# Layer 0 of a two-layer image network: how the last 42 channels are laid over the partitions

## The chip, the cores and the metric

The kernel runs on one core of a Trainium2 chip, in single precision. The metric is the time of one execution on the device, in microseconds (us), and the median of several executions. A core has five engines that run side by side, each through its own list of instructions in order: TensorE (PE in the profile; its weight loads are PEld) multiplies matrices, VectorE (DVE) and ScalarE (ACT) work on elements, GpSimd (POOL) does a little of the same, and SyncE (SP) issues the DMA transfers. Engines wait for each other by semaphores. TensorE writes to PSUM, a memory of 128 partitions and eight banks; everything else lies in SBUF, with 128 partitions too. A matmul takes a weight block (contracted rows on the partitions, by output columns) and a moving block, and writes its output columns to PSUM partitions.

## The reference, cut to what matters

The input x has shape (4, 64, 256, 256): four images of 64 channels. The change lies in layer 0 alone:

```
x = x + L0(gn(x))                     # gn: normalise by groups of 2 channels

h = einsum('oi,bihw->bohw', w_in, x)  # 64 -> 3 * 170 channels
gate, x_sp, x_fr = split(h, 3, axis=1)
sp = depthwise conv 3x3 of x_sp with w_dw, padding SAME
f  = rfft2 of x_fr in 8x8 patches, times fft_weight
fr = irfft2(f)
fused = gelu(gate) * (sp + fr)
L0 = einsum('oi,bihw->bohw', w_out, fused)   # 170 -> 64 channels
```

Layer 1, which follows, normalises again and runs two bidirectional state-space scans, along rows and along columns, with a feed-forward part. Nothing of it is touched.

## The kernel before

Layer 0 goes through each image in 32 strips of eight rows, 128 strips in all. The 170 hidden channels fall into groups of 64, 64 and 42. The first two groups ("a") share the partitions, and their convolution is done as products on TensorE (products). The group of 42 ("b") is laid out so that both halves of the partitions hold the same 42 channels (padded to 64) for different rows of the strip, and its 3x3 convolution is nine multiply-and-add instructions ("taps") over 128 partitions: the first by ScalarE, the other eight by VectorE (tap_b, L858).

The rows of x come in by parity. load_rows (L653) loads into at[0:64] every second row from one above the strip, and into at[64:128] the rows between; er holds the same kind of rows without the shift, and en is er normalised. Group b keeps this order before the change: one partition half has the strip's even rows, the other its odd ones.

The steps of group b are these. inputs_b (L751) multiplies at by xb, which holds the weights of the filter input on a block diagonal, in four matmuls over all 128 rows to 64 columns, 512 wide; half of each weight block is zero. ScalarE copies the result to rows 1 to 4 of xat, and two DMAs copy shifted rows of each half to the other half of a second tile, xen, from which taps 3, 4 and 5 (the middle row of the filter) read. Row 0 of xat is the last row of the strip before, copied by ScalarE in normal_rows (L681). gate_b (L847) does the same for the gate with gw, from en, and ScalarE puts its Gelu into geb. inverse_b (L831) turns the spectrum back with the table qi2, and add_b (L843) adds it to the taps' sum, acc. fuse_b (L869) multiplies with geb, and project (L875) multiplies acc by w_out and adds the part of the other groups in the same PSUM tile, from which residual (L888) adds er.

The strips overlap. The loop at L944 writes out one order of work by hand for the strip at hand (cur), the next (ahead) and the one before (behind); the instructions of TensorE, VectorE and ScalarE keep that order on their queues (mm at L203, vec and act at L161). The order of the DMAs on SyncE's queue is left to the framework's scheduler. Within an iteration it begins with tap 0, and the parts that matter here stand in this order: products of the first half with spec1 of the next strip, gate_a, inverse_b, project of the strip before, inverse_a, spec2 of the next strip (parts 0 and 1), products of the second half, inverse_a, gate_b, inputs_b of the next strip, tap 5, spec2 of the next strip (part 2).

PSUM is full: two tiles of two banks each for the products (m14, m23), and two rotating buffers of two banks under the name "two", which every other matmul of the loop uses in turn. A step that takes a "two" waits until the step two before it has been read out by ScalarE or VectorE.

Of the kernel before, what the change touches and what calls it, by code (L numbers as in the profile page):

```python
# [11 lines left out]
AF = mybir.ActivationFunctionType  # L12
ALU = mybir.AluOpType
# [3 lines left out]
C = 64  # L17
HID = 170
S = 256
P = 128  # L20
# [38 lines left out]
def _constants():  # L59

    out = np.zeros((P, CONST_N), np.float64)

    def put(name, a):
        o, w = CONST_AT[name]
        out[: a.shape[0], o : o + w] = a

    eye = np.eye(P)
    swap = np.roll(eye, C, axis=0)
    put("ident", eye)
    put("swap", swap)  # L70
    put("nswap", -swap)
    put("cen", eye - np.kron(np.eye(2), np.full((C, C), 1.0 / C)))
    pair = np.kron(np.eye(C // 2), np.ones((2, 2)))
    put("gm", np.kron(np.ones((2, 2)), pair) / 4.0)
    put("on2", np.kron(np.eye(2, 34, 2), np.full((C, 1), 1.0 / C)))
    put("sgn", np.concatenate([-np.ones((C, 1)), np.ones((C, 1))]))

    r, c = np.meshgrid(np.arange(8), np.arange(8), indexing="ij")  # L80
    q, sel = [], []
    for k1 in range(8):
        for k2 in range(5):
            own = k1 in (0, 4) and k2 in (0, 4)
            if k2 in (0, 4) and k1 > 4:
                continue
            w = np.zeros(40)
            w[k1 * 5 + k2] += 0.5
            w[((8 - k1) % 8 if k2 in (0, 4) else k1) * 5 + k2] += 0.5
            ang = 2 * np.pi * (k1 * r + k2 * c) / 8  # L90
            q.append(np.cos(ang).ravel() / 8 * (1 if own else math.sqrt(2)))
            sel.append(w)
            if not own:
                q.append(np.sin(ang).ravel() / 8 * math.sqrt(2))
                sel.append(w)
    q, sel = np.array(q), np.array(sel)
    assert q.shape == (64, 64) and np.allclose(q @ q.T, np.eye(64))
    put("qf", np.concatenate([q.T, q.T]))
    qi2 = np.zeros((2, 64, 2, 4, 2, 8))
    for pc in range(2):  # L100
        qi2[pc, :, :, :, pc] = q.reshape(64, 4, 2, 8).transpose(0, 2, 1, 3)
    put("qi2", qi2.reshape(128, 128))
    put("qj", qi2.reshape(128, 2, 4, 8, 2).transpose(0, 1, 4, 2, 3).reshape(128, 128))
    put("selt", np.concatenate([sel, sel]).T)
    return out.astype(np.float32)

# [2 lines left out]
def tile_kernel(ctx: ExitStack, tc: tile.TileContext, x, cst, w0, winp, wdwp, w1, out):  # L109
    nc = tc.nc  # L110
    nb = x.shape[0]

    def new(pool, shape, tag, bufs=None, dt=F32):
        return pool.tile(shape, dt, tag=tag, name=tag, **({} if bufs is None else {"bufs": bufs}))
# [49 lines left out]
    vec, act, gps = InOrder(nc.vector), InOrder(nc.scalar), InOrder(nc.gpsimd)  # L164
# [27 lines left out]
    with ExitStack() as l0:  # L192
# [10 lines left out]
        def mm(*args, **kw):  # L203

            tc.keep_in_program_order(nc.tensor.matmul(*args, **kw))  # L205

        gw = wt0("gw").rearrange("p (g m) -> p g m", g=3)
        ow = wt0("ow").rearrange("p (g m) -> p g m", g=3)
        ga, oa = new(wp, [P, P], "ga"), new(wp, [P, C], "oa")
        for h in range(2):  # L210
            p = slice(h * C, (h + 1) * C)
# [5 lines left out]
        xb = new(wp, [P, P], "xb")  # L217
        taps = new(wp, [P, 9], "taps")
        with tc.tile_pool(name="prep0", bufs=1) as prep:
# [4 lines left out]
            lo, hi, every = slice(0, C), slice(C, P), slice(0, P)  # L224
# [26 lines left out]
        with tc.tile_pool(name="pssp", bufs=1, space=PSUM) as pp:  # L251
            ps = new(pp, [P, 512], "sp")
# [380 lines left out]


        ats = [new(ld, [P, 5, S + 2], f"at{k}", 1) for k in range(3)]
        xats = [new(wk, [P, 5, S + 2], f"xat{k}", 1) for k in range(2)]
        for t in ats + xats:
            nc.gpsimd.memset(t[:, :, 0 : S + 2 : S + 1], 0.0)

# [41 lines left out]
        def normal_rows(n):  # L681
            t = strips[n]
            b, s, at = t["b"], t["s"], t["at"]
            if s == 0:
                out_stats[b] = new(wk, [P, 2 * NS0, 6], "stats2")
            lo, hi = (1 if s == 0 else 0), (4 if s == NS0 - 1 else 5)
            normalise(at[:, lo:hi, 1 : S + 1], at[:, lo:hi, 1 : S + 1], b)
            if s == 0:
                nc.gpsimd.memset(at[0:C, 0, 1 : S + 1], 0.0)
                normalise(at[C:P, 0, 1 : S + 1], at[C:P, 0, 1 : S + 1], b, slice(C, P))  # L690
            if s == NS0 - 1:
                nc.gpsimd.memset(at[C:P, 4, 1 : S + 1], 0.0)  # L692
                normalise(at[0:C, 4, 1 : S + 1], at[0:C, 4, 1 : S + 1], b, slice(0, C))
            en = t["en"] = new(wk, [P, 4, S], "en")
            normalise(en, t["er"], b)

            v14 = t["v"] = new(wk, [P, 5, S], "v14")
            t["v14"], t["v23"] = v14.rearrange("p r (c k) -> p r k c", k=2), new(wk, [P, 5, 2, 128], "v23")
            t["xat"], t["xen"] = xats[n % 2], new(wk, [P, 4, S + 2], "xen")
            t["hw"], t["stats2"] = hws[n % 2], out_stats[b]  # L700
            if s > 0:
                act.copy(t["xat"][:, 0], strips[n - 1]["xat"][:, 4])

        def outer_in(t):

# [44 lines left out]

        def inputs_b(t):  # L751

            if t["s"] == 0:
                ps = new(pp, [P, 2, 512], "two").rearrange("p q (r c) -> p (q r) c", c=S)
                mm(ps[:, 0], lhsT=xb, rhs=t["at"][:, 0, 1 : S + 1], start=True, stop=True)
                act.copy(t["xat"][:, 0, 1 : S + 1], ps[:, 0])
            ps = new(pp, [P, 2, 512], "two").rearrange("p q (r c) -> p (q r) c", c=S)
            for i in range(2):
                for h in range(2):
                    p = slice(h * C, (h + 1) * C)  # L760
                    mm(
                        ps[p, 2 * i : 2 * i + 2], lhsT=xb[:, p], rhs=t["at"][:, 1 + 2 * i : 3 + 2 * i, 1 : S + 1],
                        start=True, stop=True,
                    )
            act.copy(t["xat"][:, 1:5, 1 : S + 1], ps)
            for k in range(2):
                nc.sync.dma_start(out=t["xen"][k * C : (k + 1) * C], in_=t["xat"][(1 - k) * C : (2 - k) * C, k : k + 4])

        def products(t, half, name, third):

# [43 lines left out]
        def outer(t, half):  # L814
            y = t["y", half] = t.pop("y").rearrange("p e k x -> p (e k x)")
            vec.tensor_tensor(y, t.pop("m14").rearrange("p e k m c -> p (e k m c)"), y, ALU.add)
# [28 lines left out]
            vec.tensor_tensor(o, t.pop("fr").rearrange("p f (m c) -> p f m c", m=4), o, ALU.add)  # L845

        def gate_b(t):  # L847
            ps = new(pp, [P, 2, 512], "two").rearrange("p q (r c) -> p (q r) c", c=S)
            for i in range(2):
                for h in range(2):  # L850
                    p = slice(h * C, (h + 1) * C)
                    mm(
                        ps[p, 2 * i : 2 * i + 2], lhsT=gw[:, 2, p], rhs=t["en"][:, 2 * i : 2 * i + 2, :], start=True, stop=True
                    )
            t["geb"] = new(wk, [P, 4, S], "geb", 1)
            act.activation(t["geb"], ps, AF.Gelu)

        def tap_b(t, k):  # L858
            dy, dx = k // 3, k % 3
            src = (t["xat"][:, 0:4], t["xen"], t["xat"][:, 1:5])[dy]  # L860
            if k == 0:
                t["acc"] = new(wk, [P, 4, S], "acc")
                act.activation(t["acc"], src[:, :, dx : dx + S], AF.Copy, scale=taps[:, 0:1])
                return
            vec.scalar_tensor_tensor(
                t["acc"], src[:, :, dx : dx + S], taps[:, k : k + 1], t["acc"], ALU.mult, ALU.add
            )

        def fuse_b(t):  # L869
            vec.tensor_tensor(t["acc"], t["acc"], t["geb"], ALU.mult)  # L870
# [1 line left out]
        def split(v, half):  # L872
            return v.rearrange("p m (c k) -> p k m c", k=2)[:, :, :, half * 64 : (half + 1) * 64]

        def project(t):  # L875
            po = t["po"] = new(pp, [P, 2, 512], "two")
            for half in range(2):
                fu = t.pop(("fu", half))
                for e in range(2):
                    p = slice(e * C, (e + 1) * C)  # L880
                    mm(
                        po[p, half].rearrange("p (k m c) -> p k m c", k=2, m=4), lhsT=ow[:, 2, p], rhs=split(t["acc"], half),
                        start=True, stop=False,
                    )
                for e in range(2):
                    mm(po[e * C : (e + 1) * C, half], lhsT=oa, rhs=fu[:, e], start=False, stop=True)

# [56 lines left out]
        for b in range(nb):  # L944
            if b + 1 < nb:
                nxt_stats = new(wk, [P, 2 * NS0, 6], "stats1")
            for s in range(NS0):
# [11 lines left out]
                def ahead(step, *args):  # L959
                    if nxt is not None:  # L960
                        step(nxt, *args)
# [37 lines left out]
                behind(finish, 0)  # L999
                inverse_a(cur, 0)  # L1000
                outer(cur, 0)
                ahead(spec2, 0)
                ahead(spec2, 1)
                behind(finish, 1)
# [12 lines left out]
                inverse_a(cur, 1)  # L1017
                outer(cur, 1)
                gate_b(cur)
                ahead(inputs_b)  # L1020
                tap_b(cur, 5)
                ahead(spec2, 2)
                if s == NS0 - 3 and b + 1 < nb:
# [600 lines left out]
```

## Time and profile before

| | us |
|---|---|
| median of 3 runs | 9118.38 |
| lowest and highest run | 9117.01, 9126.76 |
| the profiled execution's own time | 9128.26 |
| its span | 9126.5 |
| first and last tap 0 of layer 0 in it, from the span's start | 182.1, 4146.2 |
| VectorE, one tap (128 partitions, 1024 elements) | 1.28 |
| ScalarE, copy of the filter input to xat | 1.02 |
| DMA of xen, two per strip, 258 KB each, from issue to landing | 4.8 |

The profile lists one execution, instruction by instruction. A row of the view in order of time gives the start from the span's start, the length, the engine, the source line, the operation, what is written and read (by the names of the tiles), the shapes, and how many instructions were merged. Matmuls overlap, so the length of a merged run of matmuls is longer than what it adds; from the start of one run to the start of the next is what it takes. L205 and L301 are the lines of the helpers that record matmuls and VectorE's operations, so rows are told apart by their tiles. One row covers instructions of the same kind that follow without a pause.

### The profile page before, as it was taken

Reading aid. Unit: us, or ns where it says so; the run is one execution under the profiler, and the core shown is the slowest. Engines: PE = TensorE matmul, PEld = TensorE weight load, DVE = VectorE, ACT = ScalarE, POOL = GpSimd, SP = SyncE. Lnnn points to the kernel's source line nnn. Section 1 sums busy time; section 2 is a strip of 40 time slices with the busy share of each in tenths; the row PEclk is TensorE's granted clock in tenths of the full one; section 3 lists DMA queues with packets and bytes.
Section 4 is the critical chain, followed back from the end, with each engine's and each line's share of the span. In section 5 each row is a group of like instructions: output and inputs, shape, how many; then the busy total and the mean of one; then the engine's idle time right before and its main releaser. Section 6 shows DMA issues by size and latency. Waiting matters only on the chain. (4 is left out here: it accounts for less than half of the span.)

```text
span 9126.5 us, 182410 instructions
## 1 busy us (share of the span) xinstructions
PE 8613.1 (94%) x78454; PEld 5705.4 (63%) x78454; DVE 7105.8 (78%) x8837; ACT 3460.7 (38%) x5218; POOL 2406.8 (26%) x1278
## 2 busy tenths in 40 slices
PE   3999999999999999998899988999978999889999
PEld 2666666666666666665566656566655666555666
DVE  7999999999999998896766756677756677567676
ACT  3444444444444444445422236222254222352222
POOL 3000000000000000003734435544446444455443
PEclk9999999999999999999999999999999999999999
DMA  7444444444444333334423335233253233451332
GB/s 175 107 107 107 104 105 110 109 103 105 108 107 107 92 93 87 91 85 134 147 57 88 85 103 177 73 80 88 70 170 113 70 89 80 117 187 40 88 84 70
DMA packets 655573, 938.37 MB, mean 103 GB/s; under 512 B 43184, under 2 KB 584880, under 8 KB 619184
## 3 DMA queue, kind: packets, MB, share of 16 engines
q1 hardware_dynamic: 654768, 926.71, 38.3%
q8 instruction: 618, 10.13, 0.5%
q14 instruction: 187, 1.53, 0.1%
HBM read 583.86 MB, written 275.05 MB: 94 GB/s over the span
## 5 line engine op out<-in xcount | busy, mean ns | idle before, releaser
L205 PE MATMUL m<-v,sw 64*128 64x256 f32 (+1 forms) x8192 | 1538.6, 392 | 0.1
L205 PEld LDWEIGHTS m<-v,sw 64*128 64x128 f32 (+1 forms) x8192 | 1120.0, 187 | 503.2 <-issue 360.0
L1439 POOL TENSOR_TENSOR xr<-xr,fx 128x512 f32<-128x512 f32 x512 | 651.5, 1272 | 1864.4 <-ACT xr L1438 1375.5
L1344 PE MATMUL pst<-fx,wb 64*128 64x256 f32 (+1 forms) x4992 | 1019.8, 438 | 37.8 <-DVE stm L301 18.3
L692 POOL MEMSET at<- 64x256 f32 x4 | 1.2, 308 | 3685.1 <-PE two L205 3685.1
L301 DVE SCALAR_TENSOR_TENSOR acc<-xat,taps,acc 128x1024 f32<-128x1024 f32 x640 | 820.6, 1282 | 15.3 <-ACT acc L162 1.6
L1344 PEld LDWEIGHTS pst<-fx,wb 64*128 64x128 f32 (+1 forms) x4992 | 508.9, 187 | 374.6 <-issue 245.3
L1469 POOL TENSOR_TENSOR rs<-ve,mhalf 128x32 f32<-128x32 f32 x128 | 695.5, 5434 | 100.5 <-DVE ve L301 100.5
L162 ACT ACTIVATE ge<-two 128x1024 f32<-128x1024 f32 x256 | 262.7, 1026 | 1080.1 <-PE two L205 1080.0
L301 DVE SCALAR_TENSOR_TENSOR stm<-stm,step,pst 128x512 f32<-128x512 f32 x640 | 478.6, 748 | 232.5 <-PE pst L1344 219.0
L1440 ACT ACTIVATE sq<-xr 128x512 f32<-128x512 f32 x512 | 323.4, 632 | 876.4 <-POOL xr L1439 876.4
L205 PEld LDWEIGHTS m<-ct,hw 128*64 128x64 f32 x16384 | 509.3, 138 | 118.1 <-issue 118.1
L301 DVE SCALAR_TENSOR_TENSOR sto<-sto,step,pst 128x512 f32<-128x512 f32 x512 | 382.9, 748 | 242.5 <-PE pst L1344 231.2
L1344 PE MATMUL px<-wb,xr 128*128 128x128 f32 x4096 | 567.8, 282 | 0.0
L301 DVE TENSOR_TENSOR z<-xc,pr 128x512 f32<-128x512 f32 x256 | 265.1, 1037 | 386.2 <-PE pr L1100 378.8
L301 DVE TENSOR_TENSOR hw<-two,wsp 128x1020 f32<-128x1020 f32 (+1 forms) x384 | 422.7, 1101 | 176.0 <-PE two L205 162.7
L1344 PEld LDWEIGHTS px<-wb,xr 128*128 128x128 f32 x4096 | 518.0, 192 | 54.2 <-issue 41.8
L301 DVE TENSOR_TENSOR y<-px,rs 128x512 f32<-128x512 f32 x512 | 354.2, 692 | 226.5 <-PE px L1344 217.2
L1344 PE MATMUL ph<-sto,wb 128*64 128x128 f32 (+1 forms) x5120 | 528.0, 299 | 0.0
L205 PE MATMUL m<-ct,hw 128*64 128x64 f32 x16384 | 527.1, 223 | 0.0
L1344 PE MATMUL ph<-stm,wb 128*64 128x128 f32 (+1 forms) x5120 | 525.0, 299 | 0.0
L1344 PEld LDWEIGHTS ph<-stm,wb 128*64 128x64 f32 (+1 forms) x5120 | 408.9, 147 | 144.6 <-issue 128.0
(317 smaller groups left out, 16420.7 us busy)
## 6 DMA issues: line engine op xcount, KB each, us to landing
strip<-x1d SPq DMA_DIRECT2D x512, 256.0 KB, 7.5
fx<-fxd SPq DMA_DIRECT2D x128, 1024.0 KB, 7.0
at<-in_x_dram SPq DMA_DIRECT2D x248, 320.0 KB, 5.4
xen<-xat SPq DMA_DIRECT2D x256, 258.0 KB, 4.8
sx<-in_x_dram SPq DMA_DIRECT2D x256, 256.0 KB, 4.0
pr<-in_x_dram SPq DMA_DIRECT2D x256, 256.0 KB, 4.1
er<-in_x_dram SPq DMA_DIRECT2D x256, 256.0 KB, 4.1
x1d<-x SPq DMA_DIRECT2D x256, 256.0 KB, 4.0
```

Source lines behind the costliest of these rows:

```text
L162: return lambda *args, **kw: tc.keep_in_program_order(getattr(self.engine, name)(*args, **kw))
L205: tc.keep_in_program_order(nc.tensor.matmul(*args, **kw))
L301: tc.keep_in_program_order(getattr(nc.vector, name)(*args, **kw))
L692: nc.gpsimd.memset(at[C:P, 4, 1 : S + 1], 0.0)
L1344: tc.keep_in_program_order(nc.tensor.matmul(*args, **kw))
L1439: nc.gpsimd.tensor_tensor(xr, xr, fx, ALU.add)
L1440: nc.scalar.activation(sq, xr, AF.Square)
L1469: nc.gpsimd.tensor_tensor(r, ve.rearrange("p n c -> p (n c)"), mhalf, ALU.pow)
```

## The change

Group b now lies by half of the strip: the lower partition half holds the first four of eight consecutive rows, the upper half the last four. Since at and en hold rows by parity, each matmul of inputs_b and gate_b now takes one parity's half of the partitions (64 rows) and writes to one half of the output partitions (64 columns), two rows at a time: four 64x64 tiles, each with its own quarter of the array, the two parities in two banks. ScalarE's copy and Gelu interleave the two parities as they write. xat grows from five rows to six, with two rows of overlap at its top: the upper half gets them from the lower half's last rows, the lower half from the upper half of the strip before, each by a DMA. All nine taps now read xat at a row offset, so xen and its two DMAs go, and so does ScalarE's copy of one row. In project, acc is no longer in er's order, so each matmul with the b weights splits in two of half the width, by the partition half that holds the rows. The table qi2 is reordered to match. In the loop, inputs_b of the next strip moves up, from after gate_b to ahead of spec2 (part 0).

```
-        xats = [new(wk, [P, 5, S + 2], f"xat{k}", 1) for k in range(2)]
+        xats = [new(wk, [P, 6, S + 2], f"xat{k}", 1) for k in range(2)]
...
-            t["xat"], t["xen"] = xats[n % 2], new(wk, [P, 4, S + 2], "xen")
+            t["xat"], t["last"] = xats[n % 2], xats[1 - n % 2]
...
-            if s > 0:
-                act.copy(t["xat"][:, 0], strips[n - 1]["xat"][:, 4])
...
         def inputs_b(t):
+            xat = t["xat"]
+            lo, hi = slice(0, C), slice(C, P)
...
+                nc.sync.dma_start(out=xat[lo, 0:2], in_=t["last"][hi, 4:6])
...
-            for i in range(2):
-                for h in range(2):
-                    p = slice(h * C, (h + 1) * C)
+            for e in range(2):
+                for o in range(2):
+                    p = slice(e * C, (e + 1) * C)
                     mm(
-                        ps[p, 2 * i : 2 * i + 2], lhsT=xb[:, p], rhs=t["at"][:, 1 + 2 * i : 3 + 2 * i, 1 : S + 1],
+                        ps[o * C : (o + 1) * C, e], lhsT=xb[p, p], rhs=t["at"][p, 1 + 2 * o : 3 + 2 * o, 1 : S + 1],
                         start=True, stop=True,
                     )
-            act.copy(t["xat"][:, 1:5, 1 : S + 1], ps)
-            for k in range(2):
-                nc.sync.dma_start(out=t["xen"][k * C : (k + 1) * C], in_=t["xat"][(1 - k) * C : (2 - k) * C, k : k + 4])
+            act.copy(
+                xat[:, 2:6, 1 : S + 1].rearrange("p (j e) c -> p e j c", e=2), ps.rearrange("p e (j c) -> p e j c", j=2)
+            )
+            nc.sync.dma_start(out=xat[hi, 0:2], in_=xat[lo, 4:6])
...
         def gate_b(t):
...
-                        ps[p, 2 * i : 2 * i + 2], lhsT=gw[:, 2, p], rhs=t["en"][:, 2 * i : 2 * i + 2, :], start=True, stop=True
+                        ps[o * C : (o + 1) * C, e], lhsT=gw[p, 2, p], rhs=t["en"][p, 2 * o : 2 * o + 2, :], start=True, stop=True
...
         def tap_b(t, k):
-            src = (t["xat"][:, 0:4], t["xen"], t["xat"][:, 1:5])[dy]
+            src = t["xat"][:, dy : dy + 4, dx : dx + S]
...
         def project(t):
...
-                for e in range(2):
-                    p = slice(e * C, (e + 1) * C)
-                    mm(
-                        po[p, half].rearrange("p (k m c) -> p k m c", k=2, m=4), lhsT=ow[:, 2, p], rhs=split(t["acc"], half),
-                        start=True, stop=False,
-                    )
+                for h in range(2):
+                    for e in range(2):
+                        mm(
+                            po[e * C : (e + 1) * C, half].rearrange("p (k m c) -> p k m c", k=2, m=4)[:, :, 2 * h : 2 * h + 2],
+                            lhsT=ow[:, 2, h * C : (h + 1) * C], rhs=split(t["acc"][:, e::2], half), start=(h == 0), stop=False,
+                        )
...
                 outer(cur, 0)
+                ahead(inputs_b)
                 ahead(spec2, 0)
                 ahead(spec2, 1)
...
                 gate_b(cur)
-                ahead(inputs_b)
                 tap_b(cur, 5)
                 ahead(spec2, 2)
```

More of the change, by code (lines that the diff above doesn't have):

```diff
@@ L101, in _constants @@
         qi2[pc, :, :, :, pc] = q.reshape(64, 4, 2, 8).transpose(0, 2, 1, 3)
+    put("qj", qi2.reshape(128, 2, 4, 8, 2).transpose(0, 1, 4, 2, 3).reshape(128, 128))
+    for pc in range(2):
+        qi2[pc, :, :, :, pc] = q.reshape(64, 2, 4, 8)
     put("qi2", qi2.reshape(128, 128))
-    put("qj", qi2.reshape(128, 2, 4, 8, 2).transpose(0, 1, 4, 2, 3).reshape(128, 128))
     put("selt", np.concatenate([sel, sel]).T)
@@ L751, in inputs_b @@
         def inputs_b(t):
+            xat = t["xat"]
+            lo, hi = slice(0, C), slice(C, P)
             if t["s"] == 0:
[L754 to L757, printed above, removed]
-            for i in range(2):
-                for h in range(2):
-                    p = slice(h * C, (h + 1) * C)
+                ps = new(pp, [P, 2, 512], "two")
+                mm(ps[lo, 0, :S], lhsT=xb[hi, hi], rhs=t["at"][hi, 0, 1 : S + 1], start=True, stop=True)
+                act.copy(xat[lo, 1, 1 : S + 1], ps[lo, 0, :S])
+                nc.gpsimd.memset(xat[lo, 0, 1 : S + 1], 0.0)
+            else:
+                nc.sync.dma_start(out=xat[lo, 0:2], in_=t["last"][hi, 4:6])
+            ps = new(pp, [P, 2, 512], "two")
+            for e in range(2):
+                for o in range(2):
+                    p = slice(e * C, (e + 1) * C)
                     mm(
-                        ps[p, 2 * i : 2 * i + 2], lhsT=xb[:, p], rhs=t["at"][:, 1 + 2 * i : 3 + 2 * i, 1 : S + 1],
+                        ps[o * C : (o + 1) * C, e], lhsT=xb[p, p], rhs=t["at"][p, 1 + 2 * o : 3 + 2 * o, 1 : S + 1],
                         start=True, stop=True,
                     )
-            act.copy(t["xat"][:, 1:5, 1 : S + 1], ps)
-            for k in range(2):
-                nc.sync.dma_start(out=t["xen"][k * C : (k + 1) * C], in_=t["xat"][(1 - k) * C : (2 - k) * C, k : k + 4])
+            act.copy(
+                xat[:, 2:6, 1 : S + 1].rearrange("p (j e) c -> p e j c", e=2), ps.rearrange("p e (j c) -> p e j c", j=2)
+            )
+            nc.sync.dma_start(out=xat[hi, 0:2], in_=xat[lo, 4:6])
         def products(t, half, name, third):
@@ L847, in gate_b @@
         def gate_b(t):
[L848 to L851, printed above, removed]
+            ps = new(pp, [P, 2, 512], "two")
+            for e in range(2):
+                for o in range(2):
+                    p = slice(e * C, (e + 1) * C)
                     mm(
-                        ps[p, 2 * i : 2 * i + 2], lhsT=gw[:, 2, p], rhs=t["en"][:, 2 * i : 2 * i + 2, :], start=True, stop=True
+                        ps[o * C : (o + 1) * C, e], lhsT=gw[p, 2, p], rhs=t["en"][p, 2 * o : 2 * o + 2, :], start=True, stop=True
                     )
             t["geb"] = new(wk, [P, 4, S], "geb", 1)
-            act.activation(t["geb"], ps, AF.Gelu)
+            act.activation(
+                t["geb"].rearrange("p (j e) c -> p e j c", e=2), ps.rearrange("p e (j c) -> p e j c", j=2), AF.Gelu
+            )
         def tap_b(t, k):
             dy, dx = k // 3, k % 3
-            src = (t["xat"][:, 0:4], t["xen"], t["xat"][:, 1:5])[dy]
+            src = t["xat"][:, dy : dy + 4, dx : dx + S]
             if k == 0:
                 t["acc"] = new(wk, [P, 4, S], "acc")
-                act.activation(t["acc"], src[:, :, dx : dx + S], AF.Copy, scale=taps[:, 0:1])
+                act.activation(t["acc"], src, AF.Copy, scale=taps[:, 0:1])
                 return
-            vec.scalar_tensor_tensor(
-                t["acc"], src[:, :, dx : dx + S], taps[:, k : k + 1], t["acc"], ALU.mult, ALU.add
-            )
+            vec.scalar_tensor_tensor(t["acc"], src, taps[:, k : k + 1], t["acc"], ALU.mult, ALU.add)
         def fuse_b(t):
@@ L878, in project @@
                 fu = t.pop(("fu", half))
-                for e in range(2):
-                    p = slice(e * C, (e + 1) * C)
-                    mm(
-                        po[p, half].rearrange("p (k m c) -> p k m c", k=2, m=4), lhsT=ow[:, 2, p], rhs=split(t["acc"], half),
-                        start=True, stop=False,
-                    )
+                for h in range(2):
+                    for e in range(2):
+                        mm(
+                            po[e * C : (e + 1) * C, half].rearrange("p (k m c) -> p k m c", k=2, m=4)[:, :, 2 * h : 2 * h + 2],
+                            lhsT=ow[:, 2, h * C : (h + 1) * C], rhs=split(t["acc"][:, e::2], half), start=(h == 0), stop=False,
+                        )
                 for e in range(2):
```

## The prediction, made before the changed kernel was run

> **What bounds it now.** I read the page first, then busy time by stretch, then one strip in order of time on each engine, then the waits. The page (busy time, share of the span, instructions) says TensorE, with VectorE second:
>
> ```profile
> span 9126.5 us, 182410 instructions
> PE 8613.1 (94%) x78454; PEld 5705.4 (63%) x78454; DVE 7105.8 (78%) x8837; ACT 3460.7 (38%) x5218; POOL 2406.8 (26%) x1278
> ```
>
> The busy times by stretch (length, then PE, PEld, DVE, ACT, POOL, granted clock, DMA share, GB/s), one row per image of layer 0; images one, three and four:
>
> ```profile
> 182.00:1176.00 994.00, 988.51 (x11226) 652.89 (x11226) 923.10 (x958) 423.52 (x480) 1.19 (x3) 1.00 0.45 108
> ...
> 2173.00:3170.00 997.00, 992.41 (x11240) 652.64 (x11240) 927.24 (x963) 423.05 (x479) 1.17 (x3) 1.00 0.43 105
> 3170.00:4180.00 1010.00, 1004.84 (x11348) 660.43 (x11345) 904.78 (x911) 421.33 (x477) 0.31 (x1) 1.00 0.35 85
> ```
>
> TensorE is busy 99.5% at full clock, VectorE 93%. The last image has no statistics of a next one, so VectorE is lighter there, yet strips are no shorter. So TensorE sets the strip: 31.03 us, from project to project (2000.09 to 2031.12). The change touches only these 128 strips. One strip's TensorE, runs in order of time (start, length, x counts; each fp32 matmul is two records):
>
> ```profile
> 2003.61 2.03 PE L205 MATMUL m<-ct,hw 128*64 128x64 f32 x64
> 2005.57 1.94 PE L205 MATMUL two<-hs,ct 64*64 64x510 f32 x16
> 2007.44 1.13 PE L205 MATMUL m<-v,sw 64*128 64x256 f32 x8
> ...
> 2014.69 2.08 PE L205 MATMUL m<-ct,hw 128*64 128x64 f32 x64
> 2016.61 1.89 PE L205 MATMUL two<-en,w0t 128*64 128x512 f32 x8
> 2018.33 1.89 PE L205 MATMUL two<-at,xb 128*64 128x512 f32 x8
> 2020.15 0.80 PE L205 MATMUL two<-hs,ct 64*64 64x340 f32 x8
> 2020.88 1.13 PE L205 MATMUL m<-v,sw 64*128 64x256 f32 x8
> ```
>
> Read start to start, since ends overlap: gate_b 1.72, inputs_b 1.82. Each is four 512-column matmuls, two abreast. The second row is eight matmuls of the form that the change uses (64 rows by 64 columns, 510 wide): 1.87, so 0.93 for four. Four run abreast: in the single records they start within 0.02 us, and the next four 0.43 later.
>
> VectorE in the same strip (in brackets, idle before, and what ended it), then ScalarE, then SyncE's queue:
>
> ```profile
> 2013.61 1.29 DVE L301 TENSOR_TENSOR y<-m,m 128x512 f32<-128x512 f32 x2 [0.30 <-ACT m L162]
> ...
> 2018.55 1.28 DVE L301 SCALAR_TENSOR_TENSOR acc<-xen,taps,acc 128x1024 f32<-128x1024 f32 x1
> 2021.02 0.87 DVE L301 TENSOR_TENSOR hw<-two,wsp 128x680 f32<-128x680 f32 x1 [1.20 <-PE two L205]
> ...
> 2028.13 1.29 DVE L301 TENSOR_TENSOR y<-m,m 128x512 f32<-128x512 f32 x2 [0.23 <-ACT m L162]
> ```
>
> ```profile
> 2009.61 1.02 ACT L162 ACTIVATE ge<-two 128x1024 f32<-128x1024 f32 x1 [8.34 <-PE two L205]
> ...
> 2020.27 1.01 ACT L162 COPY xat<-two 128x1024 f32<-128x1024 f32 x1 [0.70 <-PE two L205]
> 2021.32 1.15 ACT L162 ACTIVATE acc<-xat,taps 128x1024 f32<-128x1024 f32 x1
> ```
>
> ```profile
> 2006.89 1.27 SPq L902 DMA_DIRECT2D x1d<-x  x2
> 2020.26 0.62 SPq L665 DMA_DIRECT2D at<-in_x_dram  x1
> 2021.31 1.14 SPq L767 DMA_DIRECT2D xen<-xat  x2
> ```
>
> VectorE's waits of a strip on others are 0.30, 0.23 and 1.20, 1.73 in all. Without them it needs 31.03 - 1.73 = 29.30. That is the second floor, close under the first.
>
> **Part by part, per strip.**
>
> *Gate and filter input.* gate_b to the next products took 2016.61 to 2020.88, 4.27. After: gate_b as four tiles, 512 columns, 0.86 (two steps of 0.43), then spec2(2) 0.72: 1.58, so 2.69 less. inputs_b returns ahead of spec2(0) at 0.86. Net -1.83.
>
> Here a rule speaks against the change. The Trainium skill, "TensorEngine Tiling (Array Packing)", Key Properties, says that changing the tiling mode drains TensorE. The trace agrees: from the last four tiles (start 2006.93, plus 0.43) to the next products at 2007.44 is 0.09. If each new run of 64x64 tiles paid on both sides, four changes would cost 0.36 and leave -1.47. But each stands next to a spec2 of the same mode: today's changes, 128x64 to 64x64 to 64x128, stay two at each place. I take zero.
>
> *The evacuation.* The same page, PSUM Bottleneck, says tiling speeds TensorE but not the emptying of PSUM. That decides something here. The two-bank PSUM buffers "two" rotate between two; spec2(1), second after inputs_b, needs inputs_b's buffer back from ScalarE. If inputs_b starts at T, its second four start at T+0.48 and end 0.59 later; ScalarE starts 0.05 after (2020.21 to 2020.27 today), takes 1.01, and TensorE resumes some 0.07 later: T+2.20. spec2(0) is through at T+0.91+0.86 = T+1.77. So a new wait of 0.43. Low end 0 (were the buffer free in time), high end 0.43; I take 0.35, as VectorE's lag may already hold spec2(0) a little. The cover: ScalarE idles 8.34 before ge, so the copy finds it free; without that cover up to a 1.0 us activation would stand ahead. Queued behind the waiting matmul is all of TensorE, so it counts in full.
>
> Elsewhere the rotation eases: spec2(2) no longer needs geb's release. spec2(0) now needs residual's, which is done at 2005.48 against 2006.48.
>
> *project.* Four matmuls of 512 become eight of 256 on the same 128x64 tiles: same columns, four more pairs of weight loads at 0.14. A pair streams 256 columns for 0.21, which hides them; exposed they cost 4 x 0.14 = 0.55. Both ends 0 and 0.55; the nearest row, 256-column products at 0.97 for four on half tiles against 0.98 for two of 512 (gate_a), says zero. I take 0.05.
>
> *ScalarE.* The 128x258 copy of a row goes (0.40, beside TensorE: zero). xat's copy and the Gelu write permuted rows in runs of 256; hs's copy permutes today and takes 1.01 for 1020, so no price. tap 0 no longer follows the xat copy, it waits for rows by DMA.
>
> *VectorE.* Same instructions; taps from xat 1.282 against xen 1.278, three of them: +0.01.
>
> *DMA.* Two issues stay two (0.57 each on SyncE), each with half the rows: 129 KB in place of 258. Moved past, on SyncE, are x1d's stores and the loads of er, pr, sx and at. Rows are ready after ScalarE's copy, about 2007.7; issue 1.1 and landing 4.8 give 2013.6. Tap 0 is wanted about 2020. Some 6 us of slack hide it. POOL gets a memset of one row in four strips of 128: nothing. The table edit only permutes constants.
>
> *Sum.* 31.03 - 1.83 + 0.35 + 0.05 = 29.60, 0.30 above VectorE's floor; VectorE's 1.20 wait for spec2(2) disappears, and late next is again TensorE. Gain 1.43 a strip, 183 us over 128. Against the profiled execution's own 9128.3 (span 9126.5 and 1.8 around it) that is 8945; the median of the runs shown is 9.9 lower, so 8935. I say **8935**.
>
> **Rivals.** *VectorE becomes the bound.* Its waits for the product copies (0.53 in this strip) hang on a TensorE-ScalarE-VectorE chain which the change leaves, and fu can wait for ge in the same way (0.3). 29.30 + 0.83 = 30.13, gain 0.90, 115 us: about 9003. For: 93% busy. Against: a late VectorE finds those copies finished. The images would then differ, the fourth being shorter.
>
> *The tiles don't run four abreast.* The new order issues both column halves of a row half in turn, spec2 alternates row halves. Two abreast leaves 1.72 and 1.82 as they are: with the wait on ScalarE, 0 to 0.35 a strip, 9118 to 9163. For: no row has this order. Against: the hardware has shown all four tiles at work with the same banks.
>
> *Slower: the copied rows land late.* SyncE's queue is in order. Were these DMAs queued behind the load of at, which waits for VectorE's outer_in (end 2017.5), they would land 0.6 + 1.1 + 4.8 = 6.5 after that. Tap 0 (1.2 with its signal) stands on ScalarE with the hs copies, and so TensorE, behind it; VectorE then needs, from tap 1 (2022.93) to the next outer_in's end (2017.5 + 31.03 = 2048.5), 25.6. That closes a ring of 6.5 + 1.2 + 25.6 = 33.3 a strip, 2.3 over today's, 294 us: 9412. It decides once the rows land more than 6.5 - 2.3 = 4.2 after outer_in's end. For: a load of at stands ahead of xen today. Against: that queue follows the time at which each transfer is released, and these rows are now released ten us before at.
>
> **How the numbers follow.** A measurement tells 0.2%, 18 us. Chances: as forecast 0.68; VectorE bound 0.18; not abreast 0.05 (0.02 of it within 0.2%); late rows 0.09 (0.02 of it late by so little that a gain is left, 0.01 near zero). Faster 0.68 + 0.18 + 0.02 = 0.88; within 0.2% 0.02 + 0.01 = 0.03; slower 0.03 + 0.06 = 0.09. Low end: no new wait and project free, 1.83 x 128 = 234, which is 8884; both at once are unlikely, so 8890. High end: the VectorE rival and a little, 9010. Beyond it lie the other two rivals, 0.14, and a tail. Both unknown prices at their high ends, 1.83 - 0.43 - 0.55 = 0.85 a strip, also end there (9009).
>
> **What would show it.** Right: gate_b and inputs_b as 64*64 rows, four starting together, 0.86 from start to start; a TensorE wait of about 0.4 on xat's copy before spec2(1); VectorE's 1.20 before hw gone; strips of 29.6 in all four images. Wrong: pairs 0.43 apart; tap 0 waiting on a DMA; VectorE without idle time while TensorE waits for it.

## The result, and the profile after

The change makes the kernel faster. Beside runs of the kernel before on the same chip (median 9118.8 us), the changed kernel takes 8969.4 us in the median; the ratio is 0.9831, with a 95% interval from 0.9819 to 0.9843. That is a gain of 149 us where 183 were forecast; 8935 was predicted, with a range of 8890 to 9010.

The head of the page for the changed kernel (busy time, share of the span, instructions):

```profile
span 8967.0 us, 184750 instructions
PE 8424.2 (94%) x79478; PEld 5727.6 (64%) x79478; DVE 7092.5 (79%) x8837; ACT 3404.5 (38%) x5094; POOL 2408.0 (27%) x1282
```

TensorE's busy time is down by 189 us, VectorE's by 13. Then the busy times of the changed kernel by stretch (length, then PE, PEld, DVE, ACT, POOL, granted clock, DMA share, GB/s), for the third and fourth image:

```profile
2086.00:3050.00 964.00, 952.07 (x11534) 662.02 (x11532) 928.89 (x968) 412.27 (x452) 1.47 (x4) 1.00 0.41 101
3050.00:4020.00 970.00, 957.94 (x11696) 670.33 (x11694) 907.48 (x913) 407.96 (x446) 0.31 (x1) 1.00 0.33 80
```

TensorE is now busy 98.8% and VectorE 96.4% of the third image: both close to full. A strip takes 29.79 us, in all four images alike, against 31.03 before; only the first two strips of the layer and those around the changes of image differ. As the fourth image, which gives VectorE less to do, is no shorter, VectorE doesn't set the strip.

The rows of TensorE by their tiles: m<-v,sw are the products, m<-ct,hw is inverse_a, two<-en,w0t gate_b, two<-at,xb inputs_b, two<-en,ga gate_a, two<-fu,oa the end of project, and two<-hs,ct spec2, the second step of the transform of the next strip (parts 0 and 1 are 510 wide, part 2 is 340 wide; hs is what ScalarE copied of the first step). VectorE's hw<-two reads spec2 out, and x<-two,er is residual. One strip of the changed kernel on TensorE, in order of time (start, length, x counts):

```profile
1499.30 1.09 PE L207 MATMUL two<-en,w0t 64*64 64x512 f32 x8
...
1514.66 2.03 PE L207 MATMUL m<-ct,hw 128*64 128x64 f32 x64
1516.62 1.09 PE L207 MATMUL two<-at,xb 64*64 64x512 f32 x8
1517.65 2.31 PE L207 MATMUL two<-hs,ct 64*64 64x510 f32 x16
1519.89 1.13 PE L207 MATMUL m<-v,sw 64*128 64x256 f32 x8
...
1527.07 2.09 PE L207 MATMUL m<-ct,hw 128*64 128x64 f32 x64
1529.09 1.09 PE L207 MATMUL two<-en,w0t 64*64 64x512 f32 x8
1530.00 0.75 PE L207 MATMUL two<-hs,ct 64*64 64x340 f32 x8
1530.68 1.14 PE L207 MATMUL m<-v,sw 64*128 64x256 f32 x8
```

From start to start: the strip, from gate_b to gate_b, takes 1499.30 to 1529.09, 29.79. gate_b with spec2 part 2 now takes 1529.09 to 1530.68, 1.59 in place of 4.27. inputs_b takes 1.03 where it stands, and the two parts of spec2 after it 2.24, where they took 1.87. In the single records the four tiles of inputs_b start at 1516.62 to 1516.64, all within 0.02, and the next four 0.48 later. The same stretch on the other engines shows what the 2.24 holds: ScalarE's copy, and the weight loads that wait for it.

```profile
1517.81 1.02 ACT L164 COPY xat<-two 128x1024 f32<-128x1024 f32 x1 [5.81 <-PE two L207]
...
1518.87 0.21 PEld L207 LDWEIGHTS two<-hs,ct 64*64 64x64 f32 x8 [1.01 <-ACT xat L164]
```

The copy ends at 1518.82 and TensorE goes on at 1518.87. VectorE's rows of this strip that answer to those shown of before:

```profile
1502.38 0.86 DVE L303 TENSOR_TENSOR hw<-two,wsp 128x680 f32<-128x680 f32 x1
...
1526.04 1.29 DVE L303 TENSOR_TENSOR y<-m,m 128x512 f32<-128x512 f32 x2 [0.59 <-ACT m L164]
```

The wait of 1.20 before hw has gone. One of the two waits for the copy of m has gone too; the other is 0.59 long. The row copies on SyncE, and tap 0 that needs them on ScalarE:

```profile
1519.56 0.56 SPq L773 DMA_DIRECT2D xat<-xat  x1
```

```profile
1531.16 1.14 ACT L164 ACTIVATE acc<-xat,taps 128x1024 f32<-128x1024 f32 x1
```

The copy is issued at 1519.56; with the median landing of 3.8 it is there more than 7 us before tap 0 starts, and tap 0 shows no idle time before it.

### The profile page after: what moved, and what is told of

Same layout as the page of the kernel before. It is cut to its first block, busy times and chain, and to the rows that moved or that the text cites. A ratio compares the mean times of both kernels' runs of the same rounds, so it can differ in the third digit from the quotient of the medians.

```text
span 8967.0 us, 184750 instructions
## 1 busy us (share of the span) xinstructions
PE 8424.2 (94%) x79478; PEld 5727.6 (64%) x79478; DVE 7092.5 (79%) x8837; ACT 3404.5 (38%) x5094; POOL 2408.0 (27%) x1282
## 5 line engine op out<-in xcount | busy, mean ns | idle before, releaser
L303 DVE SCALAR_TENSOR_TENSOR acc<-xat,taps,acc 128x1024 f32<-128x1024 f32 x1024 | 1311.5, 1281 | 16.6 <-ACT acc L164 2.9
L1475 POOL TENSOR_TENSOR rs<-ve,mhalf 128x32 f32<-128x32 f32 x128 | 695.3, 5432 | 99.2 <-DVE ve L303 99.2
L164 POOL TENSOR_TENSOR rs<-ve,mhalf 128x32 f32<-128x32 f32 x64 | 347.7, 5433 | 566.0 <-DVE ve L303 554.3
L1350 PEld LDWEIGHTS ph<-sto,wb 128*64 128x64 f32 (+1 forms) x5120 | 405.0, 147 | 143.0 <-issue 129.8
```

Of the source, the lines that this page charges most:

```text
L164: return lambda *args, **kw: tc.keep_in_program_order(getattr(self.engine, name)(*args, **kw))
L303: tc.keep_in_program_order(getattr(nc.vector, name)(*args, **kw))
L1475: nc.gpsimd.tensor_tensor(r, ve.rearrange("p n c -> p (n c)"), mhalf, ALU.pow)
```

## The experiments

The theory is that the gain is TensorE's alone: four tiles abreast in place of two in gate_b and inputs_b, less what the new place of inputs_b costs in waits. The rivals are that the smaller transfers, the dropped copy or the new order bring it; that the form of the tile matters rather than the number abreast; and that VectorE now sets the strip.

**The tile form undone, all else kept (e1).**

```
-  ps[o * C : (o + 1) * C, e], lhsT=xb[p, p], rhs=t["at"][p, 1 + 2 * o : 3 + 2 * o, 1 : S + 1],
+  ps[o * C : (o + 1) * C, e], lhsT=xb[:, p], rhs=t["at"][:, 1 + 2 * o : 3 + 2 * o, 1 : S + 1],
...
-  ps[o * C : (o + 1) * C, e], lhsT=gw[p, 2, p], rhs=t["en"][p, 2 * o : 2 * o + 2, :], start=True, stop=True
+  ps[o * C : (o + 1) * C, e], lhsT=gw[:, 2, p], rhs=t["en"][:, 2 * o : 2 * o + 2, :], start=True, stop=True
```

> The changed kernel with the tile form alone undone: gate_b and inputs_b multiply over all 128 rows again (zero-padded weights, same outputs, same places in the order). Theory (the gain is four tiles abreast on TensorE): each of the two takes 0.86 us a strip more, minus 0.12 as spec2 no longer catches VectorE's residual; 29.79 to about 31.4 a strip, 9165 to 9190 us in all, so slower than before the change, since the wait of spec2 on ScalarE's copy of xat (0.37) stays. Rival (the gain comes from the smaller DMAs, the dropped ScalarE copy and the order of work, TensorE's tiles are hidden): stays within 20 us of the changed kernel's 8969.

It took 9142.9 us, ratio to before 1.0028 (1.0017 to 1.0039). One strip on TensorE:

```profile
1501.56 1.06 PE L207 MATMUL two<-en,ga 64*128 64x512 f32 x4
...
1513.59 1.89 PE L207 MATMUL two<-at,xb 128*64 128x512 f32 x8
1515.41 2.27 PE L207 MATMUL two<-hs,ct 64*64 64x510 f32 x16
1517.62 1.13 PE L207 MATMUL m<-v,sw 64*128 64x256 f32 x8
...
1532.86 1.06 PE L207 MATMUL two<-en,ga 64*128 64x512 f32 x4
```

From gate_a to gate_a the strip is 31.30, 1.51 more than with four tiles. The forecast said 31.4 and 9165 at least, so both came out too high: the strip by 0.1, and the time also because every strip of the layer was taken to scale alike (see the changes of image below). The direction is settled: without the tile form the change is a small loss. The rival that the transfers or the order bring the gain falls. spec2 is still 2.21 long here, so most of that wait comes with the place of inputs_b and not with the tiles.

**Only gate_b undone (e2)**, by the second of those edits.

> The changed kernel with gate_b alone back on 128 rows by 64 columns. Theory: 0.86 a strip more, less 0.10 for a change of tiling mode that moves from before gate_b to after it, and 0.10 again there: net 0.86, so 30.6 a strip and 9075 to 9085 us; the fourth image like the others. Rival (VectorE, busy 96%, now sets the strip): less than half of it shows, under 9025.

It took 9058.3 us, ratio 0.9938 (0.9923 to 0.9953).

```profile
1500.00 2.08 PE L207 MATMUL m<-ct,hw 128*64 128x64 f32 x64
1501.92 1.89 PE L207 MATMUL two<-en,w0t 128*64 128x512 f32 x8
...
1520.20 1.09 PE L207 MATMUL two<-at,xb 64*64 64x512 f32 x8
1521.11 1.03 PE L207 MATMUL two<-hs,ct 64*64 64x510 f32 x8
1522.45 1.08 PE L207 MATMUL two<-hs,ct 64*64 64x510 f32 x8 [0.31 <-ACT xat L164]
1523.47 1.13 PE L207 MATMUL m<-v,sw 64*128 64x256 f32 x8
...
1530.65 2.08 PE L207 MATMUL m<-ct,hw 128*64 128x64 f32 x64
```

The strip is 30.65, 0.86 more, as expected; the time is some 20 us under the expected one, in good part for the same reason as in e1. More than half of it shows, so TensorE sets the strip also here. And inverse_a ahead of gate_b takes 1.92 when the same tiling mode follows, against 2.02 (1527.07 to 1529.09 above) when 64x64 tiles follow. This 0.10 is missing in the prediction's sum. inputs_b takes 0.91 here in place of 1.03, and spec2 2.36 in place of 2.24: together 3.27 in both kernels.

**Two 64x64 tiles in the old layout (e3).**

```
-  ps[p, 2 * i : 2 * i + 2], lhsT=xb[:, p], rhs=t["at"][:, 1 + 2 * i : 3 + 2 * i, 1 : S + 1],
+  ps[p, 2 * i : 2 * i + 2], lhsT=xb[p, p], rhs=t["at"][p, 1 + 2 * i : 3 + 2 * i, 1 : S + 1],
...
-  ps[p, 2 * i : 2 * i + 2], lhsT=gw[:, 2, p], rhs=t["en"][:, 2 * i : 2 * i + 2, :], start=True, stop=True
+  ps[p, 2 * i : 2 * i + 2], lhsT=gw[p, 2, p], rhs=t["en"][p, 2 * i : 2 * i + 2, :], start=True, stop=True
```

> The kernel before, with gate_b and inputs_b on 64x64 tiles in its own layout: only the two tiles on the diagonal are used (each parity's rows to its own output half). Theory (what counts is how many tiles run abreast): two abreast as before, so 31.04 a strip, 9119 us, within 20. Rival (the 64x64 form, or the half of the rows being zeros, is what costs): as much faster as the change, 8950 to 8990.

It took 9123.2 us, ratio 1.0001 (0.9992 to 1.0009): no difference. gate_b's run, by its start and that of the next run:

```profile
1519.15 1.93 PE L205 MATMUL two<-en,w0t 64*64 64x512 f32 x8
1520.92 1.88 PE L205 MATMUL two<-at,xb 64*64 64x512 f32 x7
```

It takes 1.77 for the same eight records that take 0.91 with four abreast. The forecast held. The form alone brings nothing; the new layout is what gives all four quarters of the array something to do. (In the second row one record of eight is listed apart.)

**The move alone, in the kernel before (e4).**

```
                 outer(cur, 0)
+                ahead(inputs_b)
                 ahead(spec2, 0)
...
                 gate_b(cur)
-                ahead(inputs_b)
```

> The kernel before with one edit: inputs_b of the next strip moved up ahead of spec2 part 0. Theory: TensorE's work is the same and the move costs the wait of spec2 part 1 on ScalarE's copy, 0.37, less 0.08 which gate_a no longer waits: 31.3 a strip, 9150 to 9160 us. Rival (the move is part of the gain, since VectorE's 1.20 wait for spec2 part 2 goes): faster than before by 20 us or more.

It took 9142.4 us, ratio 1.0029 (1.0018 to 1.0039): slower, 31.29 a strip, as the theory had it, with the time 8 us under.

```profile
1515.39 2.27 PE L205 MATMUL two<-hs,ct 64*64 64x510 f32 x16
1517.59 1.14 PE L205 MATMUL m<-v,sw 64*128 64x256 f32 x8
```

spec2 takes 2.20 here too. And e4 and e1 are the same in strip (31.29 and 31.30) and time (9142.4 and 9142.9): all that the change does besides tiles and move, the transfers, the dropped copy, the taps' source and project, is worth nothing that can be told.

**inputs_b back at its old place, in the changed kernel (e5)**, the reverse of that edit.

> The changed kernel with inputs_b of the next strip back at its old place, after gate_b. Theory (the move is what hides the row copies): xat is ready some 3.2 us after gate_b starts, issue and landing of the row copy take 4.4 more, so tap 0 starts 5.6 later than in the changed kernel (7.7 in place of 2.1 after gate_b's start); ScalarE's hs copies queue behind it and gate_a's PSUM buffer with them, 4.5 us past its time, less the 0.5 of waits that the old place doesn't have: about 33.8 a strip, 9450 to 9500 us. Rival (the landing is hidden anyway): 8969 less those 0.5 a strip, 8905 to 8925.

It took 9412.5 us, ratio 1.0315 (1.0298 to 1.0333): the loss that the theory forecast, but some 40 us under its range. ScalarE, SyncE and TensorE at the end of a strip:

```profile
1525.56 1.01 ACT L164 COPY xat<-two 128x1024 f32<-128x1024 f32 x1
1529.84 1.15 ACT L164 ACTIVATE acc<-xat,taps 128x1024 f32<-128x1024 f32 x1 [3.28 <-DMA xat<-xat]
```

```profile
1525.45 0.62 SPq L667 DMA_DIRECT2D at<-in_x_dram  x1
1526.59 0.50 SPq L773 DMA_DIRECT2D xat<-xat  x1
```

```profile
1531.94 1.17 PE L207 MATMUL two<-en,ga 64*128 64x512 f32 x4 [1.72 <-ACT hs L164]
```

Tap 0 waits for the rows, hs behind it, and TensorE for hs. From the first tap 0 to the last, at 183.8 and 4444.0, the 127 strips between take 33.55 in the mean (33.8 forecast), and they are uneven, 31.7 to 36.7, where nearly all strips of the other kernels agree within 0.1 outside the changes of image. Two things make them uneven. The rows land 2.3 to 5.2 us after their issue. And in many strips TensorE's clock is halved for a time behind its wait. Here are two strips in a row, from tap 0 to tap 0, the second beginning with the tap 0 above (columns as in the stretches of the result, so the granted clock is the third number from the end):

```profile
1496.35:1529.84 33.49, 31.36 (x362) 21.70 (x360) 29.02 (x30) 12.73 (x14) 0.00 (x0) 0.95 0.35 89
1529.84:1561.88 32.04, 30.03 (x364) 20.64 (x362) 28.94 (x30) 12.73 (x14) 0.00 (x0) 1.00 0.36 96
```

A granted clock of 0.95 over 33.49 us is a loss of 1.7: half the clock for 3.4 us. Of the 108 strips away from the ends and from the changes of image, the trace shows no such loss in 38, 1.7 us in 60 and 3.4 in 10; from tap 0 to the end of the next copy to xat these take 28.5 to 28.7, 30.1 to 30.3 and 31.2 to 31.6. The mean loss is 1.3 a strip, which the expectation didn't have. Without it a strip would take about 32.2 (an estimate, 33.5 less 1.3), so the wait for the rows itself was forecast too long: issue and landing took 3.4 us in the median, where 4.4 were forecast.

So the move costs about 0.3 a strip and is what makes the layout pay at all.

**Without the row copies (e6).**

```
-                nc.sync.dma_start(out=xat[lo, 0:2], in_=t["last"][hi, 4:6])
...
-            nc.sync.dma_start(out=xat[hi, 0:2], in_=xat[lo, 4:6])
```

> The changed kernel without its two row DMAs per strip; rows 0 and 1 of xat are set to zero once and stay so, which leaves out part of the filter's input rows. Theory (the copies are hidden): no change, 8969 within 10. Rival (late rows, or SyncE's queue held up by them, still cost part of the missing gain): 20 us or more faster.

It took 8968.0 us, ratio 0.9832 (0.9817 to 0.9846), 29.79 a strip, as the changed kernel has it: the copies are hidden wholly, and SyncE's queue plays no part in the missing gain.

**inputs_b one step further up (e7).**

```
+                ahead(inputs_b)
                 inverse_a(cur, 0)
                 outer(cur, 0)
-                ahead(inputs_b)
```

> The changed kernel with inputs_b one step further up, ahead of inverse_a of the first half. Theory: the 2 us of inverse_a then cover ScalarE's copy of xat, so the 0.37 wait of spec2 part 1 goes; two more changes of tiling mode cost 0.19 a strip: net 0.15 to 0.25 less, 8937 to 8950 us. Rival (VectorE at 96% or its residual holds spec2 in any case): the wait moves to spec2 part 0 and the time stays within 8 us of 8969, or rises by the two mode changes to 8993.

It took 8944.9 us, ratio 0.9804 (0.9789 to 0.9818).

```profile
1507.47 1.03 PE L207 MATMUL two<-fu,oa 128*64 128x512 f32 x4
1508.42 1.09 PE L207 MATMUL two<-at,xb 64*64 64x512 f32 x8
1509.44 2.09 PE L207 MATMUL m<-ct,hw 128*64 128x64 f32 x64
1511.46 1.94 PE L207 MATMUL two<-hs,ct 64*64 64x510 f32 x16
1513.33 1.13 PE L207 MATMUL m<-v,sw 64*128 64x256 f32 x8
```

spec2 is back at 1.87, and the two more changes of mode are seen: project's last run is 0.95 (0.86 before), and inputs_b 1.02 with no wait behind it (0.91 in e2, where its own mode follows). inverse_a behind it takes 2.02 in place of 1.96. The strip is 29.56, 0.23 less, inside the forecast.

**inputs_b ahead of inverse_b (e8)**, with at normalised ahead of ScalarE's copy of m, and en taken out of normal_rows into a function of its own, normal_en, behind inputs_b.

```
-                products(cur, 0, "m23", False)
                 if nxt is not None:
                     normal_rows(n + 1)
-                normal_patches(n + 2)
+                products(cur, 0, "m23", False)
                 middle(cur)
                 products(cur, 0, "m14", False)
+                ahead(inputs_b)
+                if nxt is not None:
+                    normal_en(n + 1)
+                normal_patches(n + 2)
...
                 outer(cur, 0)
-                ahead(inputs_b)
```

> The changed kernel with inputs_b ahead of inverse_b, the normalising of at ahead of ScalarE's copy of m, and that of en behind inputs_b. Theory: with project and inverse_a in between, both waits before spec2 go (0.37 on the copy of xat, 0.12 on the residual), for one or two more mode changes (0.10 to 0.19): 29.4 to 29.5 a strip, close to VectorE's floor of 29.3, so 8930 us within 12. Rival (VectorE sets the strip already): within 10 us of 8969.

It took 8929.7 us, ratio 0.9785 (0.9771 to 0.9800): the fastest, and faster than the change. Strip and time are as the theory forecast: the strip is 29.43. TensorE's spec2, and inputs_b at its new place:

```profile
1505.87 1.94 PE L207 MATMUL two<-hs,ct 64*64 64x510 f32 x16
1507.74 1.14 PE L207 MATMUL m<-v,sw 64*128 64x256 f32 x8
...
1526.88 1.09 PE L207 MATMUL two<-at,xb 64*64 64x512 f32 x8
1527.90 2.09 PE L207 MATMUL two<-ct,hw 128*64 128x64 f32 x64
```

Neither wait is left: spec2 takes 1.87 as in the kernel before, and inputs_b 1.02. VectorE, which the rival held to be the bound of the changed kernel, wasn't: in the stretch from 1120 to 1900 it is busy 762 of 780 us here, where it was 755 in the changed kernel.

## Why the prediction was right, and where it was short

The mechanism was right, and the time lies in the range; two terms of the sum were too small. The forecast was 1.43 less a strip, measured is 1.24 less, that is 31.03 to 29.79. By its terms (read from single rows, so their sum is off by 0.01):

| term, us a strip | predicted | measured |
|---|---|---|
| gate_b to the next products, 4.27 before | 1.58 | 1.59 |
| inverse_a ahead of gate_b: a change of mode | 0 | +0.10 |
| inputs_b, to the start of spec2 | 0.86 | 1.03 |
| spec2 parts 0 and 1, over 1.87 | +0.35 | +0.37 |
| project, over 3.52 | +0.05 | +0.01 |
| gate_a of the first half, 0.98 before | 0 | -0.08 |
| sum against 31.03 | -1.43 | -1.25 |

The last term but the sum is a wait that went: before, gate_a's weights waited 0.21 for VectorE's hw (at 2008.39). The prediction's price for project leaned on this 0.98, wait included; the 0.05 that it took was small enough for that not to matter.

**The tiles.** Four abreast, as the row of spec2 promised. The new order of issue, both column halves of one row half in turn, makes no difference: the four start together. gate_b takes 0.91 and part 2 of spec2 0.68, where 0.86 and 0.72 were said: the first step behind a change of mode is 0.48, not 0.43, and this 0.05 has moved from one run to the other with the change, so the sum stands. e1, e2 and e3 show that this is the gain, and e1 beside e4 that nothing else is.

**The change of tiling mode** is a step that failed, though its count was right. "I take zero" rested on two changes at each place before and after. But the stretch of 4.27 began with gate_b. Before, the change of mode came inside it, after inputs_b; after, it comes ahead of gate_b, in inverse_a's run, which the sum left out. So it was booked as saved and not as spent, 0.10 a strip, 13 us. The trace of before had its price (0.09 behind a run as the prediction counts it, from the last of the four tiles at 2006.93; 0.11 from the first, at 2006.91). The rule that the prediction cites from the Trainium skill, "TensorEngine Tiling (Array Packing)", Key Properties, that a change of tiling mode drains TensorE, agrees with the 0.10 measured here.

**The wait for ScalarE's copy** was worked out as 0.43, taken as 0.35, and came out as 0.54, which is the larger miss: 0.19 a strip, 24 us. The rows of inputs_b and of spec2 in the table belong together: 1.03 + 2.24 is 3.27, where 0.86 + 1.87, 2.73, had no wait in it. By steps (T is the start of inputs_b, 1516.62): the second four tiles start at T+0.48 as said, the copy begins at T+1.18 (1.12 said), TensorE goes on at T+2.25 (2.20 said) and needs 1.02 more, where the working left some 0.96: behind the stop, too, the second four tiles follow the first after 0.48.

The prediction took less than its 0.43 because VectorE's lag might already hold spec2 part 0. It did: part 0 starts 0.12 later than T+0.91, for its buffer waits for VectorE's residual, which ends at 1517.51 by the trace, when inputs_b's last tiles have been streamed at about 1517.53. The prediction saw this release a full microsecond early ("done at 2005.48 against 2006.48"). The likely reason is that VectorE runs later against TensorE, which no longer gives it 1.20 of idle time a strip; in e2, with more time for VectorE, the residual ends at 1520.22, 0.9 before part 0 needs it. But this wait costs nothing by itself, and saves nothing: e2 doesn't have it and takes the same 3.27, for the copy ends last in both.

e8 takes both waits away: inputs_b and spec2 take 1.02 + 1.87, 2.89 in place of 3.27, with one change of mode more in it. gate_a takes 0.93 in place of 0.90, so the strip should be 29.44, and 29.43 was measured.

**VectorE as the bound** was wrong for this change. Its floor of 29.30 was a little high: 29.79 less the one wait of 0.59 is 29.20, and in e8 29.43 less the one wait of 0.36 is 29.07. It bounds what is still to be had, not the strip.

**The changes of image** are a term that the prediction lacked; it took 128 strips at one price. Five strips around each change cost 7.5, 7.4 and 6.7 more than five common ones before, and 10.3, 11.2 and 7.3 in the changed kernel, 7 us in all. There TensorE stops for results which VectorE must first come to. After the first image, the changed kernel, and then the kernel before:

```profile
1062.40 1.95 PE L207 MATMUL two<-hs,ct 64*64 64x510 f32 x16 [1.81 <-DVE x L303]
...
1078.09 0.53 PE L150 MATMUL two<-var,ct 128*128 128x1 f32 x2 [1.99 <-DVE var L147]
```

```profile
1099.78 1.09 PE L205 MATMUL two<-hs,ct 64*64 64x510 f32 x8 [0.74 <-DVE x L301]
...
1116.70 0.35 PE L148 MATMUL two<-var,ct 128*128 128x1 f32 x2 [0.83 <-DVE var L145]
```

With VectorE later in its list, both stops are longer: the one for residual is 1.81 in place of 0.74, the one for the statistics 1.99 in place of 0.83. And behind the stop of 1.99 TensorE's clock is halved for 3.4 or 6.8 us, at all three changes of the changed kernel; the kernel before has this at the third change alone. The strip that follows, in the changed kernel at the first change, then in the kernel before at the first and at the third (granted clock third from the end):

```profile
1075.56:1110.32 34.76, 32.26 (x368) 23.06 (x370) 28.72 (x34) 13.12 (x16) 0.88 (x2) 0.95 0.31 73
```

```profile
1115.47:1148.46 32.99, 32.14 (x360) 21.46 (x362) 28.63 (x34) 13.55 (x17) 0.57 (x1) 1.00 0.35 85
3117.11:3151.74 34.63, 33.80 (x362) 22.90 (x364) 28.62 (x34) 13.54 (x17) 0.55 (x1) 0.95 0.35 81
```

The halved clock loses 6.8 us at the three changes in place of 1.7, so it can be up to 5 of the 7 us. In e1 and e2, where TensorE is slower, these strips cost 13 and 17 us in all, 16 and 12 less than the 29 in the changed kernel, which is a good part of what their times fell under the forecasts. From the first tap 0 to the last the two traces differ by 155 us: 127 strips at 1.25 (31.04 before, from tap 0 to tap 0) are 159, the changes of image take 7 off, and the first two strips of the layer, 57 in the changed kernel in place of 62, give some 3 back. That the medians differ by 149 is within what single executions differ (8964 to 8973 for the changed kernel, 9117 to 9127 before).

**The late rows** didn't come, as the queue's order by time of release had suggested. e5 shows that rows which land late hold tap 0, hs and TensorE as that rival said, when the move is taken back, but it is not the rival's ring. There the DMA was to stand behind the load of at. In e5 that load is off SyncE's queue at 1526.07, and the DMA is issued at 1526.59, when ScalarE's copy has ended at 1526.57: the ring runs from the copy over the rows, tap 0, hs and TensorE to the next inputs_b. That e5 came out at the rival's 9412 us is chance, all the more as 1.3 of its 33.55 a strip is the halved clock.

## What to carry to other kernels

A matmul whose weights are half zeros can give way to one on a quarter of the array, but what pays is the number of tiles abreast: lay the data so that all four have work, and put the new run beside one of the same mode. A step that is moved takes its turn among the rotating PSUM buffers with it; look two steps on for the one that will wait for its copy, and choose a place where a run of another buffer covers it (e8 got 0.36 a strip back so). When summing a stretch, include the run ahead of it, since a change of mode is charged to the run that ends. And read the granted clock around every stop of TensorE: here a stop could cost the time that it took and half a clock behind it.

## What the runs showed of the hardware that was not expected

TensorE's granted clock fell to a half for 3.4 us, in some places for 6.8, behind stops of TensorE, and the more often the longer the stop. In e5 TensorE waits for hs in every strip; of the 108 strips away from the ends and the changes of image, the loss of 1.7 or 3.4 us stood in 5 of the 27 with a wait of 1.5 to 1.8 us, in 26 of 39 with 1.8 to 2.0, in 12 of 15 with 2.0 to 2.5 and in all 27 with more. Behind the stop of 1.99 at the changes of image it came three times of three in the changed kernel, behind 1.31 twice of three in e1, behind 0.83 once of three in the kernel before. In the changed kernel's common strips, where TensorE's rows show no idle time over 0.14, it didn't come. What decides it in the single case is not shown.

A transfer of 129 KB from SBUF to SBUF landed 2.3 to 5.2 us after its issue in e5. In the changed kernel the same transfers have some 7 us to spare, and nearly all strips take 29.76 to 29.83.

A change of tiling mode into or out of 64x64 tiles cost 0.09 to 0.11 against running on in the same mode. The first four tiles after it, and also after a stop (1522.45 to 1522.93 in e2), are followed by the next four after 0.48 rather than 0.43.
